# A fused mixture-of-experts kernel on one Trainium2 core: an expert's down products in seven half-size products for eight, from the third pair of batch rows on

## The chip, the core and the metric

The kernel runs on one core of a Trainium2 chip. Its engines work side by side, each through its own queue in order: PE (matrix products; its weight loads are shown apart as PEld), DVE, ACT and POOL (elementwise work), and SP, which issues the DMAs. They share SBUF; PE writes its products to PSUM, which DVE and ACT can read. The metric is the device time of one execution in microseconds (us), smaller being better.

## The reference, cut to what matters

Four layers are applied to `x` of shape (16, 256, 256), each added to `x`: L0, a mixer with 16 exponential moving averages per batch row and some small matrix products; L1, an attention pooling; L2, nine experts (eight and a shared one) with gated hidden layers of 1024; L3, a hidden layer of 1024 whose last 64 output columns come from one expert per batch row. All is fp32. The change is in L2:

```python
g = jnp.einsum('bsd,edf->ebsf', h, Wg)
u = jnp.einsum('bsd,edf->ebsf', h, Wu)
expert_outs = jnp.einsum('ebsf,efd->ebsd', jax.nn.silu(g) * u, Wd)
expert_output = jnp.einsum('be,ebsd->bsd', gating_probs, expert_outs)
```

## The kernel before

**Pairs and positions.** L2 and L3 take batch rows in pairs (512 columns). The work is a plan of positions 0 to 44; position `pos` takes expert `pos % 9`. Pair 0 rides from position 0 (its two rows at first apart), pair 1 from 9 to 17, pair 2 from 14 to 22, pair 3 from 18 to 26, pair 4 from 23 to 31, pair 5 from 27 to 35, pair 6 from 32 to 40, pair 7 from 36 to 44. So most positions serve two pairs with one load of weights, and positions 41 to 44 one pair. After a pair's last expert comes its L3. One pair at one position is called a *unit* here.

**A unit** (`l2_unit`) goes through 8 chunks of 128 hidden values. Every fp32 product is taken in three passes (`mm3`, lines 102 to 104), from a rounded high part and a low part of both operands. Per chunk, PE takes gate and up (4 products of three passes, 512 columns) into PSUM tiles `pg`, `pu`; ACT takes the SiLU (line 744), DVE multiplies (745, one operand `pu` in PSUM), ACT rounds the high part (89), POOL subtracts for the low part `hh` (96). Then `down` takes two products of three passes of 512 columns into `y0`, `y1`. `down` is put on PE two chunks later (`LAG`). At the end of an expert, DVE adds `y` into `acc` with four instructions (line 792).

**Weights** come in chunks of 768 columns into a ring of 10 tiles. On its first two uses a chunk is loaded raw and split by ACT and DVE (or POOL); on the second it is stored in `keep_e`, and from then on loaded ready (line 666).

**L0 and L1** of batch row b (`traces(b)`, `pooled(b)`) are cut into steps, which `pace` lays between the chunks, so that each row is done before its pair boards. Rows 6 to 15 are worked on while positions 14 to 35 run. One row has 16 averages: for each, DVE multiplies a gate by a modulation (line 328, twice 256 columns), DVE scans it (332, twice), POOL adds it up (336). The gate tile `gp` lies in PSUM (`ps_a`), and so do the factors `decay` of the scans (`ps_l`); the other operands `mod` and `bt` lie in SBUF:

```python
decay = ps_l.tile([P, ND + 1], F32, tag="decay", name="decay")
...
ga = ps_a.tile([P, 2, S], F32, tag="ga", name=f"gp{b}")
```

PSUM has eight banks: three for `pg`/`pu`, two for `y0`, `y1`, one each for `gp`, `decay` and L0's products. The instructions of each engine stand in an order that a scheduler fixed when the kernel was built; each waits by semaphores.

Of the kernel before, what the change touches and what calls it, by code (L numbers as in the profile page):

```python
# [8 lines left out]
F32 = mybir.dt.float32  # L9
# [11 lines left out]
NE = 8  # L21
# [5 lines left out]
L0_BUFS = {"bt": 3, "tr": 3, "mod": 2, "hA": 2, "hB": 2}  # L27
SECOND = 9
APART = 5
STORE = 2  # L30
LAG = 2
BOOST = 400
HOLD = 3
# [12 lines left out]
def fused_kernel(  # L46
# [23 lines left out]
    cp = ctx.enter_context(tc.tile_pool(name="const", bufs=1))  # L70
    xin = ctx.enter_context(tc.tile_pool(name="xin", bufs=2))
    l0 = ctx.enter_context(tc.tile_pool(name="l0", bufs=1))
    ring = ctx.enter_context(tc.tile_pool(name="ring", bufs=RING))
    raws = ctx.enter_context(tc.tile_pool(name="raws", bufs=2))
    xs = ctx.enter_context(tc.tile_pool(name="xs", bufs=3))
    accp = ctx.enter_context(tc.tile_pool(name="accp", bufs=3))
    hp = ctx.enter_context(tc.tile_pool(name="hp", bufs=2))
    dram = ctx.enter_context(tc.tile_pool(name="dram", bufs=2, space=bass.MemoryType.DRAM))
    keep = ctx.enter_context(tc.tile_pool(name="keep", bufs=1, space=bass.MemoryType.DRAM))
    ps_gu = ctx.enter_context(tc.tile_pool(name="ps_gu", bufs=3, space=PSUM))  # L80
# [87 lines left out]

    decay = ps_l.tile([P, ND + 1], F32, tag="decay", name="decay")
    V.reciprocal(decay, alpha)  # L170

    bmx = cp.tile([P, 2], F32, name="bmx")
    V.tensor_reduce(bmx, bl, AX.X, ALU.max)
# [26 lines left out]
    G.iota(jrow, [[P, 2]], base=1, channel_multiplier=1)  # L200

    def later_constants():

        V.tensor_copy(vr[:, 0:1], vec[:, V_V : V_V + 1])
        low("v", vr[:, 1:2], vec[:, V_V : V_V + 1], vr[:, 0:1])
        V.tensor_copy(n2[:, 0, :], vec[:, V_WN2 : V_WN2 + 48])
        low("v", n2[:, 1, :], vec[:, V_WN2 : V_WN2 + 48], n2[:, 0, :])

        V.tensor_copy(cnt[:, 0], jrow)
        V.tensor_scalar(cnt[:, 1], cnt[:, 0], -1.0, S + 1.0, ALU.mult, ALU.add)  # L210
        V.memset(cnt[:, 2], S - 1.0)
        V.tensor_copy(ptf, pti)
        V.tensor_scalar(flag[:, 0], ptf, 0.0, None, ALU.is_equal)
        V.tensor_scalar(flag[:, 1], ptf, 1.0, None, ALU.is_equal)
        V.tensor_tensor(flag[:, 2], flag[:, 0], flag[:, 1], ALU.add)
        V.tensor_scalar(flag[:, 2], flag[:, 2], -1.0, 1.0, ALU.mult, ALU.add)

        V.tensor_scalar(kindf, flag[:, 0], -2.0, 2.0, ALU.mult, ALU.add)
        V.tensor_tensor(kindf, kindf, flag[:, 1], ALU.subtract)
        V.tensor_copy(kind_i, kindf)  # L220
        for t in range(3):
            o = cntb if t == 0 else ctmp
            V.tensor_tensor(
                o,
                flag[:, t].unsqueeze(2).to_broadcast([P, NB, 2]),
                cnt[:, t].unsqueeze(1).to_broadcast([P, NB, 2]),
                ALU.mult,
            )
            if t:
                V.tensor_tensor(cntb, cntb, ctmp, ALU.add)  # L230
# [29 lines left out]

    def traces(b):

        xr = xin_tiles.pop(b)
        xh, xl = hl(f"x_{b}", "hA")
        rnd("a", xh, xr)
# [29 lines left out]
        yield  # L295
        pg = ps_l.tile([P, 2, S], F32, tag="ps", name=f"pg{b}")

        ga = ps_a.tile([P, 2, S], F32, tag="ga", name=f"gp{b}")
        for m in range(2):
            for k in range(4):  # L300
                o = O_G + k * S + m * P
# [352 lines left out]
    ring_tiles = {}  # L654

    kept, seen_of = {}, {}

    def load_chunk(key):  # L660
        kind = key[0]
        again = (kind, key[2])
        if kind != "c" and again in kept:
            t = ring.tile([P, 2, 768], F32R, tag="w", name="w_" + "_".join(map(str, key[:2])) + f"_{key[-1]}")
            n = 768 if kind == "e" else 384
            nc.sync.dma_start(t.bitcast(F32)[:, :, :n], kept[again])
            ring_tiles[key] = t
            return
        raw = raws.tile([P, 768], F32, tag="raw", name="raw_" + "_".join(map(str, key)))
        t = ring.tile([P, 2, 768], F32R, tag="w", name="w_" + "_".join(map(str, key[:2])) + f"_{key[-1]}")  # L670
        if kind == "e":
            n = 768
            nc.sync.dma_start(raw, wexp[key[2]])
        elif kind == "f":
            n = 384
            nc.sync.dma_start(raw[:, :n], w3[key[2]])
        else:
            n = 512
            b, i = key[1], key[2]
            nc.sync.dma_start(  # L680
                raw[:, :520],
                comb[bass.ds(eregs[b], 1), i].rearrange("o p c -> (o p) c"),
            )
            if i == 0:
                V.tensor_copy(bias3[:, b : b + 1], raw[:, 512:513])
        rnd("a", t[:, 0, :n], raw[:, :n])
        e = "v"
        if kind == "e" and key[1] == 0:

            e = "g" if key[2] < 2 else "v" if key[2] < 6 else "gv"[key[2] % 2]  # L690
        elif kind == "e" and key[1] < ALONE and key[2] % 3 == 0:
            e = "g"
        low(e, t[:, 1, :n], raw[:, :n], t[:, 0, :n])
        ring_tiles[key] = t
        seen_of[again] = seen_of.get(again, 0) + 1
        if kind == "e" and seen_of[again] == STORE or kind == "f":
            d = keep.tile([P, 2, n], F32, name="keep_" + "_".join(map(str, again)))
            nc.sync.dma_start(d, t.bitcast(F32)[:, :, :n])
            kept[again] = d

    eregs = {}


    x2_tiles = {}
# [34 lines left out]
    y_of = {}  # L739

    def hidden(ps_g, ps_u, uid, bias=None):
        h = hp.tile([P, 512], F32, tag="h", name=f"h{uid}")
        if ps_u is not None:
            A.activation(h, ps_g, AF.Silu)  # L744
            last_of["h"] = V.tensor_tensor(h, h, ps_u, ALU.mult)  # L745
        else:
            A.activation(h, ps_g, AF.Gelu, bias=bias)  # L747
        t = hp.tile([P, 2, 512], F32R, tag="hh", name=f"hh{uid}", bufs=3)
        rnd("a", t[:, 0], h)
        low("g", t[:, 1], h, t[:, 0])  # L750
        return t
# [5 lines left out]
    def l2_unit(pos, cis, bs):  # L757
# [39 lines left out]

        st2.push(down)

    def l3_chunk(p, f):  # L800
        uid[0] += 1
        xt = x2_tiles[p]
        w = ring_tiles[("f", p, f)]
        q = ps_gu.tile([P, 512], F32, tag="gu", name=f"q_{uid[0]}")
        for k in range(2):
            ws = slice(k * P, (k + 1) * P)
            mm3(q, w[:, 0, ws], w[:, 1, ws], xt[:, 0, k], xt[:, 1, k], k == 0, k == 1)
        t = hidden(q, None, uid[0], bias=vec[:, V_L3B1 + f : V_L3B1 + f + 1])
        u = uid[0]
# [1 line left out]
        def down():  # L811
            if f == 0:
                y_of[0] = [ps_y.tile([P, 512], F32, tag=f"y{m}", name=f"z{m}_{u}") for m in range(2)]
            mm3(y_of[0][0], w[:, 0, 256:384], w[:, 1, 256:384], t[:, 0], t[:, 1], f == 0, f == NF - 1)
            for i in range(2):
                b = 2 * p + i
                cw = ring_tiles[("c", b, f // 4)]
                ws = slice((f % 4) * P, (f % 4 + 1) * P)
                ts = slice(i * S, (i + 1) * S)
                mm3(  # L820
                    y_of[0][1][:, ts], cw[:, 0, ws], cw[:, 1, ws], t[:, 0, ts], t[:, 1, ts],
                    f == 0 and i == 0, f == NF - 1 and i == 1, skip_group_check=True,
                )
            if f == NF - 1:
                a = acc_tiles[p]
                V.scalar_tensor_tensor(a[:, 0], y_of[0][0], vec[:, V_B2 : V_B2 + 1], a[:, 0], ALU.add, ALU.add)  # L826
                nc.sync.dma_start(out[p, :, 0], a[:, 0])
                for i in range(2):
                    b = 2 * p + i
                    ts = slice(i * S, (i + 1) * S)  # L830
                    V.scalar_tensor_tensor(  # L831
                        a[:, 1, ts], y_of[0][1][:, ts], bias3[:, b : b + 1], a[:, 1, ts], ALU.add, ALU.add
                    )
                nc.sync.dma_start(out[p, :, 1], a[:, 1])
# [16 lines left out]
    for pos in range(max(r[1] for r in rides)):  # L851
        e = pos % NX
        units = [r[2] for r in rides if r[0] <= pos < r[1]]
        for ui, bs in enumerate(units):
            for b in bs:
                boards.setdefault(b, len(plan))
            step = 2 // len(bs)
            for c in range(e * NF, (e + 1) * NF, step):
                cis = list(range(c, c + step))
# [1 line left out]
                plan.append(("l2", (pos, cis, bs), keys, keys if ui == len(units) - 1 else [], 4))  # L861
        for p in ends.get(pos, []):
            for f in range(NF):
                keys = [("f", p, f)] + [("c", b, f // 4) for b in (2 * p, 2 * p + 1)]
                plan.append(("l3", (p, f), keys, keys if f % 4 == 3 else keys[:1], 3))

# [8 lines left out]
    def prefetch(n, boost=BOOST):  # L875
        while n > 0 and nxt[0] < len(order):
            k = order[nxt[0]]
            if k[0] == "c" and k[1] not in eregs:
                eregs[k[1]] = nc.sync.value_load(eix[0:1, k[1] : k[1] + 1], min_val=0, max_val=NE - 1)
            with tc.high_priority(offset=boost) if boost else nullcontext():  # L880
                load_chunk(k)
            nxt[0] += 1
            n -= 1

# [98 lines left out]
    owed = 0.0  # L985
    for i, item in enumerate(plan):
        kind, args, _, done = item[:4]
        if kind == "l2":
            bs = args[2]
            while n_done[0] <= bs[-1]:  # L990
                step()
            l2_unit(*args)
        else:
            if args[0] not in x3_done:
                st2.flush()
# [7 lines left out]
        if not (soon[0] == "l3" and soon[1][1] < HOLD):  # L1003
            for _ in range(min(int(owed), int(rate) + 2)):
                step()
                owed -= 1
        prefetch(len(done))
    st2.flush()


# [107 lines left out]
```

## Time and profile before

| | us |
|---|---|
| three runs: median (lowest to highest) | 2840.7 (2838.91 to 2842.95) |
| the profiled execution: time | 2841.92 |
| the profiled execution: span of its instructions | 2840.2 |
| PE busy in the span | 2779.2 |
| DVE, POOL, ACT busy in the span | 1425.2, 1299.0, 1235.4 |

Busy time is the time in which at least one instruction of the engine runs; PE's products overlap in a pipeline, so that the distance from start to start says more than the duration of one. The difference of 1.7 us between time and span lies around the program. Idle time before a group of instructions is shown with what ended it ("<-"). DVE's idle time does not cost anything as long as PE does not wait for it.

### The profile page before, as it was taken

The page shows a single profiled execution, that of the slowest core. Times are in us where ns is not written, and L with a number is a line of the kernel's source. Part 1 is how long each engine was busy: PE and PEld are TensorE (multiplying, and loading weights), DVE is VectorE, ACT ScalarE, POOL GpSimd, SP SyncE. Part 2 cuts the span into 40 slices and gives each one's busy share as a digit, 9 for nine tenths or more (in the row PEclk, how much of TensorE's full clock was granted, in tenths as well). Part 3 has the DMA queues.
Part 4 walks back from the last instruction along what each step waited for, and adds up shares of the span by engine and source line. Part 5 has one row for each costly group of instructions (what it writes and reads, how often), then busy time and mean ns, then how long its engine had stood idle before and what let it go on. Part 6 is the DMA issues. An engine that isn't in the chain of part 4 may idle for free. (4 is left out here: it accounts for less than half of the span.)

```text
span 2840.2 us, 36878 instructions
## 1 busy us (share of the span) xinstructions
PE 2779.2 (98%) x13604; PEld 2335.0 (82%) x13604; DVE 1425.2 (50%) x2646; ACT 1235.4 (43%) x2043; POOL 1299.0 (46%) x986
## 2 busy tenths in 40 slices
PE   7889989999999999999999999999999999999998
PEld 4877779888888888888888888888888888888887
DVE  7888766665665364544545445453444542222222
ACT  5555544546444533435334443334433453323433
POOL 5764654544544353544534445444444443333333
PEclk9999999999999999999999999999999999999999
DMA  4444645546443533324433153331523242222552
GB/s 125 136 148 122 196 162 181 185 131 230 148 164 117 180 115 104 119 77 135 150 110 106 40 180 112 111 117 58 177 101 112 91 169 90 89 89 76 192 198 83
DMA packets 114693, 371.23 MB, mean 131 GB/s; under 512 B 12642, under 2 KB 30930, under 8 KB 114514
## 3 DMA queue, kind: packets, MB, share of 16 engines
q1 hardware_dynamic: 114082, 368.82, 39.2%
q8 instruction: 108, 1.77, 0.3%
q14 instruction: 71, 0.58, 0.1%
q10 hardware_dynamic: 432, 0.06, 0.0%
HBM read 304.62 MB, written 64.21 MB: 130 GB/s over the span
## 5 line engine op out<-in xcount | busy, mean ns | idle before, releaser
L96 POOL TENSOR_TENSOR hh<-h,hh 128x512 fp32r<-128x512 f32 x640 | 848.7, 1326 | 1317.4 <-ACT hh L89 1297.4
L745 DVE TENSOR_TENSOR h<-h,pu 128x512 f32<-128x512 f32 x576 | 393.5, 683 | 941.9 <-PE pu L104 813.0
L89 ACT ACTIVATE hh<-h 128x512 fp32r<-128x512 f32 x640 | 403.4, 631 | 936.0 <-DVE h L745 914.9
L744 ACT ACTIVATE h<-pg 128x512 f32<-128x512 f32 x576 | 342.8, 595 | 317.7 <-PE pg L104 236.5
L102 PE MATMUL pg<-x,w_e 128*128 128x512 f32 (+1 forms) x1232 | 466.3, 379 | 10.1 <-ACT h L744 3.9
L102 PE MATMUL pu<-x,w_e 128*128 128x512 f32 (+1 forms) x1232 | 464.9, 377 | 7.5 <-ACT h L744 7.4
L104 PE MATMUL pg<-x,w_e 128*128 128x512 f32 (+1 forms) x1232 | 465.3, 378 | 1.8 <-DVE w_e L96 1.4
L103 PE MATMUL y<-hh,w_e 128*128 128x512 f32 (+1 forms) x1232 | 463.7, 377 | 2.5 <-POOL hh L96 2.5
L103 PE MATMUL pg<-x,w_e 128*128 128x512 f32 (+1 forms) x1232 | 464.7, 377 | 0.8 <-POOL x L96 0.8
L103 PE MATMUL pu<-x,w_e 128*128 128x512 f32 (+1 forms) x1232 | 463.7, 376 | 0.0
L104 PE MATMUL pu<-x,w_e 128*128 128x512 f32 (+1 forms) x1232 | 463.7, 376 | 0.0
L104 PE MATMUL y<-hh,w_e 128*128 128x512 f32 (+1 forms) x1232 | 463.1, 376 | 0.0
L102 PE MATMUL y<-hh,w_e 128*128 128x512 f32 (+1 forms) x1232 | 415.2, 377 | 2.9 <-ACT hh L89 1.6
L336 POOL TENSOR_TENSOR ta<-ta,tr 128x512 f32<-128x512 f32 x225 | 308.9, 1373 | 84.4 <-DVE tr L332 72.1
L332 DVE TENSOR_TENSOR_SCAN tr<-decay,bt 128x256 f32<-128x256 f32 x450 | 284.7, 669 | 0.0
L102 PEld LDWEIGHTS pg<-x,w_e 128*128 128x128 f32 x1232 | 232.5, 189 | 53.1 <-ACT h L744 4.8
L102 PEld LDWEIGHTS pu<-x,w_e 128*128 128x128 f32 x1232 | 232.6, 189 | 51.2 <-ACT h L744 9.9
L103 PEld LDWEIGHTS y<-hh,w_e 128*128 128x128 f32 x1232 | 232.8, 189 | 46.3 <-POOL hh L96 4.6
L104 PEld LDWEIGHTS pg<-x,w_e 128*128 128x128 f32 x1232 | 232.7, 189 | 44.9 <-DVE w_e L96 2.4
L102 PEld LDWEIGHTS y<-hh,w_e 128*128 128x128 f32 x1232 | 231.5, 189 | 45.7 <-ACT hh L89 2.6
L104 PEld LDWEIGHTS y<-hh,w_e 128*128 128x128 f32 x1232 | 232.7, 189 | 41.8
L104 PEld LDWEIGHTS pu<-x,w_e 128*128 128x128 f32 x1232 | 232.5, 189 | 41.9
(279 smaller groups left out, 3220.8 us busy)
## 6 DMA issues: line engine op xcount, KB each, us to landing
w_e<-keep_e SPq DMA_DIRECT2D x216, 768.0 KB, 4.4
raw_e<-in_wexp_dram SPq DMA_DIRECT2D x144, 384.0 KB, 4.3
keep_e<-w_e SPq DMA_DIRECT2D x72, 768.0 KB, 4.3
mod<-mdd SPq DMA_DIRECT2D x120, 256.0 KB, 3.7
w_f<-keep_f SPq DMA_DIRECT2D x56, 384.0 KB, 3.5
raw_c<-in_comb_dram SPq DMA_DIRECT2D x32, 260.0 KB, 2.8
xr<-in_xT_dram SPq DMA_DIRECT2D x16, 256.0 KB, 3.7
xt<-in_x_dram SPq DMA_DIRECT2D x16, 256.0 KB, 2.7
```

Source lines behind the costliest of these rows:

```text
L89: last_of["ca"] = A.activation(out_, in_, AF.Copy)
L96: i = (V if e == "v" else G).tensor_tensor(out_, in_, h.bitcast(F32), ALU.subtract)
L102: PE.matmul(o, wh, xh, start=start, stop=False, **kw)
L103: PE.matmul(o, wh, xl, start=False, stop=False, **kw)
L104: last_of["pe"] = PE.matmul(o, wl, xh, start=False, stop=stop, **kw)
L332: V.tensor_tensor_scan(tr[:, c], decay[:, d : d + 1].to_broadcast([P, S]), bt[:, c], 0.0, ALU.mult, ALU.add)
L336: G.tensor_tensor(tacc, tacc, tr, ALU.add)
L744: A.activation(h, ps_g, AF.Silu)
L745: last_of["h"] = V.tensor_tensor(h, h, ps_u, ALU.mult)
```

## The change

From position 14 on, a unit is taken in steps j of two chunks (256 hidden values), each in two halves (`half_unit`). Gate and up are as before: 24 passes of 512 columns per j. The down product is a product of 2 by 2 blocks (two chunks by two rows of the pair; 128 by 128 weights, 256 columns), and it is taken in seven block products for eight: 21 passes of 256 columns, where 12 passes of 512 stood. For that,

- the hidden values are combined by three subtractions on DVE (tile `t`), and seven blocks of 256 are split in high and low parts (b11, b2, t13, t24) where four were;
- the weights get four sums per j (DVE, once per expert, positions 14 to 22), and are kept as two tiles per j, `g` (1024 columns) and `d` (896), in pools of three each. A second pair takes the j in reverse order, and loads j = 0 anew;
- there are four accumulators `y0` to `y3` instead of two. `y2` and `y3` take the PSUM banks of `gp` and `decay`; for rows from 6 on (`LATE`), the gate tile (`gs`) and the factors (`decay_late`) lie in SBUF;
- at the end of an expert ACT copies one block, and DVE runs two additions and five multiply-adds, where it ran four;
- `down` of one j stands behind the gate and up products of the next.

The pools of the ring (`ring`, `raws`, `hp`) are closed at position 14, and the new pools (`lw`, `lraw`, `lh`) are laid in their space. Before position 14, chunks are no longer stored.

```diff
+SEVEN = 14
+LATE = 6
...
+    decays = {False: decay, True: cp.tile([P, ND + 1], F32, name="decay_late")}
...
+        V.tensor_copy(decays[True], decay)
...
+        decay = decays[b >= LATE]
...
-        ga = ps_a.tile([P, 2, S], F32, tag="ga", name=f"gp{b}")
+        ga = ps_a.tile([P, 2, S], F32, tag="ga", name=f"gp{b}") if b < LATE else ft("ga", f"gs{b}")
...
+    def parts(t, c0, src, n):
+        rnd("a", t[:, 0, c0 : c0 + n], src)
+        low("v", t[:, 1, c0 : c0 + n], src, t[:, 0, c0 : c0 + n])
...
+            if kind == "g":
+                parts(t, 0, r0[:, :512], 512)
+                parts(t, 512, r1[:, :512], 512)
+            else:
+                a11, a21, a12, a22 = r0[:, 512:640], r0[:, 640:768], r1[:, 512:640], r1[:, 640:768]
+                sums = pools["lh"].tile([P, 4, P], F32, tag="s", name=f"sums_{e}_{j}", bufs=1)
+                V.tensor_tensor(sums[:, 0], a21, a22, ALU.add)
+                V.tensor_tensor(sums[:, 1], sums[:, 0], a11, ALU.subtract)
+                V.tensor_tensor(sums[:, 2], a11, a21, ALU.subtract)
+                V.tensor_tensor(sums[:, 3], a12, sums[:, 1], ALU.subtract)
+                parts(t, 0, a11, P)
+                parts(t, P, r1[:, 512:768], 2 * P)
+                parts(t, 3 * P, sums.rearrange("p a b -> p (a b)"), 4 * P)
...
+        def split(tag, src, n, bufs):
+            t = lh.tile([P, 2, n], F32R, tag=tag, name=..., bufs=bufs)
+            rnd("a", t[:, 0], src)
+            low("g", t[:, 1], src, t[:, 0])
+            return t
...
+        A.activation(part, pg, AF.Silu)
+        last_of["h"] = V.tensor_tensor(part, part, pu, ALU.mult)
+        if i == 0:
+            hid["b11"] = split("b", h[:, 0], S, 2)
+            return
+        t = lh.tile([P, 4, S], F32, tag="t", name=f"t{u}", bufs=1)
+        V.tensor_tensor(t[:, 0:2], h.rearrange("p (c n) s -> p c n s", n=2)[:, :, 1], h[:, 0:2], ALU.subtract)
+        V.tensor_tensor(t[:, 2], h[:, 3], t[:, 0], ALU.subtract)
+        V.tensor_tensor(t[:, 3], h[:, 2], t[:, 2], ALU.subtract)
...
+        b2 = split("hh", flat[:, 512:1024], 512, 3)
+        t13 = split("hh", tf[:, 0:512], 512, 3)
+        t24 = split("hh", tf[:, 512:1024], 512, 3)
...
+                    (y0[:, 0], True, 0, b11, 0),
+                    (y1[:, 0], True, 1, b2, 0),
+                    (y2[:, 0], True, 6, b2, 1),
+                    (y2[:, 1], False, 3, t13, 0),
+                    (y3[:, 0], True, 5, t13, 1),
+                    (y0[:, 1], False, 4, t24, 0),
+                    (y1[:, 1], False, 2, t24, 1),
...
+                A.activation(s[:, 0], y0[:, 0], AF.Copy)
+                V.tensor_tensor(s[:, 1], s[:, 0], y0[:, 1], ALU.add)
+                V.tensor_tensor(s[:, 2], s[:, 1], y3[:, 0], ALU.add)
+                add(acc[:, :, :S], y1, ca)
+                add(acc[:, :, S:], y2[:, 1:2].to_broadcast([P, 2, S]), cb)
+                add(acc[:, 0, S:], y2[:, 0], cb)
+                add(acc[:, :, S:], s[:, 1:3], cb)
+                add(acc[:, :, :S], s[:, 0:3:2], ca)
...
+        st2.flush()
+        st2.push(down)
```

## The prediction

> **What bounds the kernel now.** First the page's sums and its costliest groups (busy time, mean ns of one | idle time before them):
>
> ```profile
> PE 2779.2 (98%) x13604; PEld 2335.0 (82%) x13604; DVE 1425.2 (50%) x2646; ACT 1235.4 (43%) x2043; POOL 1299.0 (46%) x986
> ...
> L96 POOL TENSOR_TENSOR hh<-h,hh 128x512 fp32r<-128x512 f32 x640 | 848.7, 1326 | 1317.4 <-ACT hh L89 1297.4
> L745 DVE TENSOR_TENSOR h<-h,pu 128x512 f32<-128x512 f32 x576 | 393.5, 683 | 941.9 <-PE pu L104 813.0
> ...
> L336 POOL TENSOR_TENSOR ta<-ta,tr 128x512 f32<-128x512 f32 x225 | 308.9, 1373 | 84.4 <-DVE tr L332 72.1
> L332 DVE TENSOR_TENSOR_SCAN tr<-decay,bt 128x256 f32<-128x256 f32 x450 | 284.7, 669 | 0.0
> ```
>
> PE is the bound; DVE waits for PE, POOL for ACT. Then the same by stage: positions 0 to 13, 14 to 22, 23 to 35, 36 to 44, cut at the end of the last layer-3 block of each (the stretch, then PE, PEld, DVE, ACT, POOL busy, granted clock, DMA share, GB/s):
>
> ```profile
> 0.00:666.00 666.00, 616.00 (x3470) 525.58 (x3471) 486.92 (x868) 359.02 (x598) 369.13 (x269) 0.97 0.50 158
> 666.00:1352.00 686.00, 684.33 (x3258) 574.09 (x3257) 361.07 (x687) 305.46 (x505) 320.17 (x244) 1.00 0.40 134
> 1352.00:2333.00 981.00, 979.09 (x4628) 821.03 (x4627) 460.33 (x894) 399.01 (x666) 444.17 (x346) 1.00 0.34 115
> 2333.00:2840.00 507.00, 499.73 (x2254) 414.32 (x2253) 116.86 (x201) 171.87 (x277) 165.55 (x128) 1.00 0.36 120
> ```
>
> Where the change acts, PE hardly rests; what it saves there would come straight off the time, if nothing else becomes the bound. I call the three late stages A (686 us), B (981) and C (507).
>
> **What PE saves.** The timeline of PE shows start times where products of 512 and of 256 columns follow each other:
>
> ```profile
> 437.84 0.39 PE L103 MATMUL pu<-x,w_e 128*128 128x512 f32 x1
> 438.06 0.39 PE L104 MATMUL pu<-x,w_e 128*128 128x512 f32 x1
> 438.29 0.28 PE L102 MATMUL y<-hh,w_e 128*128 128x256 f32 x1
> 438.40 0.28 PE L103 MATMUL y<-hh,w_e 128*128 128x256 f32 x1
> 438.52 0.28 PE L104 MATMUL y<-hh,w_e 128*128 128x256 f32 x1
> ```
>
> Long runs give 0.227 us per 512 columns and 0.1195 per 256 (twelve of these from 438.29 to 439.72). A group (one j of one pair) has 12 x 0.227 = 2.72 us of down products before and 21 x 0.1195 = 2.51 after: 0.214 less. There are 58 pairs-at-a-position from 14 on, with 4 groups each: 232 x 0.214 = 50 us. The first 512 behind a run of 256 starts 0.24 later instead of 0.227, some 6 us in all. So PE's own saving is 44 to 50 us, and a unit goes from 8 x 18 x 0.227 = 32.7 us to 31.8. [...]
>
> **What the other engines get, and the port.** These two answers of the timeline decide my forecast. In the first, DVE scans (factor `decay` in PSUM) while POOL works: two scans take 1.26 us, as ever. In the second, DVE's operands both lie in SBUF: it starts 0.48 us behind POOL and ends 0.55 us after POOL's end; alone it takes 0.69.
>
> ```profile
> 1499.81 1.30 POOL L96 TENSOR_TENSOR hh<-h,hh 128x512 fp32r<-128x512 f32 x1 [0.61 <-ACT hh L89]
> 1500.10 1.26 DVE L332 TENSOR_TENSOR_SCAN tr<-decay,bt 128x256 f32<-128x256 f32 x2
> ```
>
> ```profile
> 1995.84 1.29 POOL L96 TENSOR_TENSOR hh<-h,hh 128x512 fp32r<-128x512 f32 x1 [3.04 <-ACT hh L89]
> 1996.32 1.36 DVE L96 TENSOR_TENSOR w_c<-raw_c,w_c 128x512 fp32r<-128x512 f32 x1 [0.54 <-ACT w_c L89]
> ```
>
> ```profile
> L96 DVE TENSOR_TENSOR w_c<-raw_c,w_c x32: 662/1057/1783, 592.0 to 2808.8; 128x512 fp32r<-128x512 f32 x32
> L366 DVE SCALAR_TENSOR_TENSOR g<-g,sm x15: 678/684/1425, 129.9 to 2295.2; 128x512 f32<-128x512 f32 x15
> ```
>
> I took every place in the trace where one DVE instruction with both operands in SBUF overlaps one POOL instruction (96): from the first start to the last end it takes the two durations alone, added, less 0.13 us (80% of them between 0.11 and 0.16). They exclude each other. DVE instructions with an operand in PSUM show nothing of it: 155 multiplies `h<-h,pu` beside POOL take 0.677 us, 421 alone 0.688. [...]
>
> So POOL's time plus DVE's time with both operands in SBUF must fit into each stage ("port time"). Durations: POOL 1.29 (median) per 512 columns, 0.71 per 256 (the weight split of 256 columns at the start); DVE 0.68 per 512, 0.42 per 256, some 0.28 per 128 (extrapolated), scans 0.633 and `bt` 0.432 back to back (284.7/450, 207.5/480).
>
> - A unit: POOL splits 3 blocks of 512 and one of 256 per j, 4 x 4.58 = 18.3 us (before 8 x 1.29 = 10.3). DVE's `t`, 0.68 + 2 x 0.42 per j, gives 6.1, and two multiply-adds from `s` 1.4 (before: none, `pu` and `y` are in PSUM). Port 25.8 against 10.3.
> - A batch row of layers 0 and 1: POOL 19 x 1.29 + 0.7 = 25.2. With gate and factors in SBUF, 34 scans (21.5) and 32 `bt` (13.8) join; small ones are 5.2. Port 65.7 against 29.7.
> - Layer 3 of a pair: POOL 10.3, DVE 4.1: 14.4, as before.
> - First preparation of a j's weights (positions 14 to 22, 36 of them): lows 0.68 x 3 + 0.42 + 0.28, four sums 1.12: 3.9 each.
>
> | stage | units, rows, layer-3 blocks | port before | port after | PE after |
> |---|---|---|---|---|
> | A | 18, 4, 2 (and 36 preparations) | 374 | 464 + 263 + 29 + 140 = 896 | 662 |
> | B | 26, 6, 3 | 483 | 671 + 394 + 43 = 1108 | 961 |
> | C | 14, 0, 2 | 171 | 361 + 29 = 390 | 489 |
>
> PE is 31.8 per unit, 11.3 per row (84 products of 256 and some small), 22 per layer-3 block; with 32.7 it gives 678, 984 and 502 for before, where the trace has 686, 981 and 507. In A and B the port needs more than PE: it becomes the bound. DVE's whole busy time in A, some 640 us, is close to PE's as well. Behind a blocked DVE instruction stand the multiplies `h<-h,pu` that PE's next down products need, so PE waits.
>
> The port sum isn't exact. A hand-over saves up to 0.13 us at either end of each POOL instruction (384 in A, 560 in B: 100 and 146 us at most). Against that, DVE's instructions with PSUM operands (8.3 us per unit, about 6 per row: 173 and 252 us) stand in the same queue, and cost whatever does not fall beside a POOL instruction. I let the two cancel, since POOL's 450 and 656 us leave room for most but not all. **Sum:** 2842 + (896 - 686) + (1108 - 981) - 14 x 0.86 in C = 3167.
>
> **The rest.** The switch of pools: the first raw load waits for the products that free the ring, and PE has some 3 to 8 us of work from there to its first use, against 4.3 us of landing and about 3 of splitting; four j's must be prepared in a row. I take 10 us (0 to 30). Loads: between the product that frees a tile of `g` or `d` and the first product on its successor stand mostly 15 to 20 us of PE work, above 8 everywhere; a kept tile lands in 4.4 us (768 KB; somewhat more for 1 MB), so nothing is late. For layer 3's `f2` there are only 2.5 to 9 us against 3.5: 5 us in all (0 to 20). Accumulators: between a pair's last down product and the next one's first stand 24 products (5.4 us), and the chain that reads `y` is 0.4 + 2 x 0.41 + 2 x 0.75 + 0.48 = 3.2; hidden in C, and inside the port's delay in A and B. In C, a j has 8.0 us of PE against 4.6 of POOL and under 5 of DVE: its saving arrives. **Forecast: 3182, say 3180 us**, counted from the profiled execution's 2841.9 (median of three 2840.7).
>
> **Rivals.** *Port-bound, as above:* hand-overs all saved gives 2842 + 110 - 22 (B is PE's again) - 12 + 15 = 2933, and with nearly a third of the PSUM instructions unhidden it is 3182 + 130 = 3310; chance 0.60 for 2970 to 3310. *Scans go free:* no row shows a scan with both operands in SBUF. If it doesn't exclude POOL, A loses 4 x 21.5 and B 129: 810 and 979, so 2842 + 124 - 2 - 12 + 15 = 2967, less half the hand-overs in A 2917; 0.18 for 2880 to 2970. *Worse:* engines in order pass the delay back and forth, with little overlap; everything in DVE's queue and POOL's one after the other would be 896 + 173 and 1108 + 252, 3600 in all; 0.09 above 3330. *The other side:* the exclusion doesn't hold for the new instructions. Then PE stays the bound, as DVE's sum alone (some 640 of 662 in A) just fits, and 2842 - 50 + 15 = 2807 results. This decides as soon as the port needs less than PE in both stages, that is, 234 us less in A; scans and `bt` together (141) are not enough, so `t` and the preparations would have to go free too. For it speaks only that no row shows these very instructions: 0.11. *The small products save nothing:* at 0.130 us each, 21 cost as much as 12 large ones, and with a free port 2842 remains; the rows say 0.1195: 0.02.
>
> Runs of this kernel tell a difference of about 0.2%. Chances: faster 0.11, same 0.02, slower 0.87. The range takes in the first two cases with a margin: 2880 to 3330.
>
> **What would show it.** In the changed profile, PE's busy share drops in A and B and not in C; scans (line 338) and `bt` (334) have means well above 0.67 and 0.47 us with maxima near 2; POOL's splits likewise rise above 1.29; PE waits for POOL `hh`, ACT `hh` and DVE `h`. Stage A ends some 200 us later against its start than before, B some 130, C some 10 earlier. Scans at 0.67 beside POOL would prove the forecast wrong, and PE at 98% everywhere the whole of it.

## The result and the profile after

The changed kernel takes 3203.3 us (median of four runs, 3198.1 to 3205.7), the kernel before, measured beside it, 2840.9. The ratio is 1.1273 (95% interval 1.1254 to 1.1293): 362 us more. The profiled execution has a span of 3202.8 us. The lines of its page that answer to those of before:

```profile
PE 2891.5 (90%) x15692; PEld 2452.2 (77%) x15692; DVE 2571.8 (80%) x3809; ACT 1490.1 (47%) x2714; POOL 1909.7 (60%) x1450
...
L338 DVE TENSOR_TENSOR_SCAN tr<-decay_late,bt 128x256 f32<-128x256 f32 x300 | 260.6, 899 | 0.0
...
L334 DVE SCALAR_TENSOR_TENSOR bt<-gs,bl,mod 128x256 f32<-128x256 f32 x320 | 255.9, 838 | 0.1
```

Before, the line of `bt` was:

```profile
L328 DVE SCALAR_TENSOR_TENSOR bt<-gp,bl,mod 128x256 f32<-128x256 f32 x480 | 207.5, 474 | 2.0 <-DMA mod<-mdd 1.8
```

DVE has gone from 50% to 80%, and its scans from 0.669 to 0.899 us, `bt` from 0.474 to 0.838. Now by stage (the stretch, then PE, PEld, DVE, ACT, POOL busy, granted clock, DMA share, GB/s), cut at the end of the same layer-3 blocks, to a microsecond or two:

```profile
0.00:663.00 663.00, 610.71 (x3443) 520.88 (x3443) 484.00 (x864) 351.86 (x589) 367.80 (x267) 0.97 0.35 105
663.00:1580.00 917.00, 769.97 (x3959) 639.08 (x3960) 815.24 (x1258) 428.75 (x827) 526.26 (x392) 0.94 0.45 159
1580.00:2698.00 1118.00, 1017.83 (x5549) 863.72 (x5548) 946.70 (x1286) 489.05 (x899) 717.56 (x554) 0.98 0.41 141
2698.00:3203.00 505.00, 493.02 (x2746) 428.53 (x2744) 325.84 (x404) 220.42 (x401) 298.03 (x239) 0.99 0.48 170
```

A grows from 687 to 917, B from 980 to 1118, C stays (506 and 505). In A DVE is busy for 815 of 917 us, PE for 770. PE's waits over the whole span (us in total, times, longest):

```profile
PE pg L105 <- DVE h L901: 67.7, 45, 4.9
PE y L105 <- ACT hh_t L92: 52.9, 61, 3.6
PE pu L105 <- ACT h L900: 30.2, 26, 3.0
PE y L105 <- DVE acc L954: 26.4, 22, 2.7
PE y L106 <- POOL hh_t L99: 26.0, 40, 1.5
```

PE waits all along one chain: the SiLU and the multiply of `h`, the split of the sums `t`, the accumulators. The first and the third line (98 us) aren't waits for data: `pg` and `pu` share three PSUM buffers (`ps_gu`), and the next gate or up product needs one that the multiply or the SiLU has read. What holds the chain up is seen in the timeline, where two scans with both operands in SBUF stand beside one POOL split: 2.25 us for the split (1.29 alone) and 2.32 for the scans (1.26 with `decay` in PSUM).

```profile
1709.36 2.25 POOL L99 TENSOR_TENSOR hh_h<-h,hh_h 128x512 fp32r<-128x512 f32 x1 [1.03 <-ACT hh_h L92]
1709.84 2.32 DVE L338 TENSOR_TENSOR_SCAN tr<-decay_late,bt 128x256 f32<-128x256 f32 x2
```

The waits are not the whole loss. PE's timeline after a wait:

```profile
705.71 0.79 PE L107 MATMUL pg<-x,w_g 128*128 128x512 f32 x1 [1.45 <-DVE w_g L99]
706.30 0.63 PE L105 MATMUL pg<-x,w_g 128*128 128x512 f32 x1
706.73 0.63 PE L106 MATMUL pg<-x,w_g 128*128 128x512 f32 x1
...
708.86 0.51 PE L105 MATMUL pu<-x,w_g 128*128 128x512 f32 x1
709.21 0.40 PE L106 MATMUL pu<-x,w_g 128*128 128x512 f32 x1
```

From 706.30 to 708.86 products of 512 columns start 0.43 us apart, and then 0.23 again. So I split PE's time in the three late stages into products at their undisturbed distance (0.2266 and 0.1195 us), waits, and the rest, slow products: 2112 + 253 + 173 us after the change; before it, 2154 + 7 + 9. The products' time falls by 42 us (counted at fixed distances, so this isn't a measured saving yet; e10 below measures it); 246 us of waits and 164 of slow products come. Of the 173 us some 70 lie where the granted clock reads 0.5. Most of the others belong to the waits: idle time counts only from the end of the product before, 0.39 us after its start (0.28 for 256 columns), so a start behind a wait comes another 0.16 us late (273 times, 46 us), and shorter holds aren't counted as waits at all (some 41 us).

### The profile page after: what moved, and what is told of

The parts are those of the page before. It is cut to its first block, busy times and chain, and to the rows that moved or that the text cites. A ratio compares the mean times of both kernels' runs of the same rounds, so it can differ in the third digit from the quotient of the medians.

```text
span 3202.8 us, 43824 instructions
## 1 busy us (share of the span) xinstructions
PE 2891.5 (90%) x15692; PEld 2452.2 (77%) x15692; DVE 2571.8 (80%) x3809; ACT 1490.1 (47%) x2714; POOL 1909.7 (60%) x1450
## 3 DMA queue, kind: packets, MB, share of 16 engines
q8 instruction: 123, 2.02, 0.3%
## 5 line engine op out<-in xcount | busy, mean ns | idle before, releaser
L99 POOL TENSOR_TENSOR hh_t<-t,hh_t 128x512 fp32r<-128x512 f32 x464 | 658.0, 1422 | 257.1 <-ACT hh_t L92 244.0
L92 ACT ACTIVATE hh_t<-t 128x512 fp32r<-128x512 f32 x464 | 292.1, 630 | 566.5 <-DVE t L910 270.2
L99 POOL TENSOR_TENSOR hh_h<-h,hh_h 128x512 fp32r<-128x512 f32 x232 | 346.8, 1495 | 267.9 <-ACT hh_h L92 254.3
L105 PE MATMUL pg<-x,w_g 128*128 128x512 f32 x928 | 383.2, 413 | 79.9 <-DVE h L901 67.7
L105 PE MATMUL pu<-x,w_g 128*128 128x512 f32 x928 | 378.4, 408 | 33.2 <-ACT h L900 30.2
L99 POOL TENSOR_TENSOR hh<-h,hh 128x512 fp32r<-128x512 f32 x176 | 243.9, 1387 | 243.3 <-ACT hh L92 215.0
L107 PE MATMUL pg<-x,w_g 128*128 128x512 f32 x928 | 374.2, 403 | 5.5 <-DVE w_g L99 5.4
L106 PE MATMUL pg<-x,w_g 128*128 128x512 f32 x928 | 375.4, 405 | 0.0
L106 PE MATMUL pu<-x,w_g 128*128 128x512 f32 x928 | 372.2, 401 | 0.0
L107 PE MATMUL pu<-x,w_g 128*128 128x512 f32 x928 | 370.2, 399 | 0.0
L99 POOL TENSOR_TENSOR b_h<-h,b_h 128x256 fp32r<-128x256 f32 x232 | 207.3, 893 | 134.5 <-ACT b_h L92 130.0
L105 PE MATMUL y<-hh_t,w_d 128*128 128x256 f32 x928 | 238.4, 295 | 53.8 <-ACT hh_t L92 52.9
L106 PE MATMUL y<-hh_t,w_d 128*128 128x256 f32 x928 | 259.8, 293 | 26.4 <-POOL hh_t L99 26.0
L338 DVE TENSOR_TENSOR_SCAN tr<-decay_late,bt 128x256 f32<-128x256 f32 x300 | 260.6, 899 | 0.0
L334 DVE SCALAR_TENSOR_TENSOR bt<-gs,bl,mod 128x256 f32<-128x256 f32 x320 | 255.9, 838 | 0.1
L107 PE MATMUL y<-hh_t,w_d 128*128 128x256 f32 x928 | 253.8, 287 | 0.0
```

The source lines that it names most:

```text
L92: last_of["ca"] = A.activation(out_, in_, AF.Copy)
L99: i = (V if e == "v" else G).tensor_tensor(out_, in_, h.bitcast(F32), ALU.subtract)
L105: PE.matmul(o, wh, xh, start=start, stop=False, **kw)
L106: PE.matmul(o, wh, xl, start=False, stop=False, **kw)
L107: last_of["pe"] = PE.matmul(o, wl, xh, start=False, stop=stop, **kw)
L334: V.scalar_tensor_tensor(bt[:, c], ga[:, c], bl[:, c, d : d + 1], mod[:, d % 2], ALU.mult, ALU.mult)
```

## The experiments

What each gave, with A and B read from its own profile (cut as above), and two shares of those stages: DVE's busy time (in it the time that a started instruction is held up), and the time in which POOL or a DVE instruction with two SBUF operands runs, counted from both timelines ("port"). The last column ("`h` held") is the mean time by which DVE starts a multiply `h` after both its inputs, the SiLU and the last product of `pu`, are there.

| run | time, us | ratio (95%) | A, us (DVE, port) | B, us (DVE, port) | `h` held in A, B, us |
|---|---|---|---|---|---|
| before | 2840.9 | 1 | 687 (53%, 52%) | 980 (47%, 48%) | 0.27, 0.18 |
| after | 3203.3 | 1.1273 (1.1254 to 1.1293) | 917 (89%, 87%) | 1118 (85%, 86%) | 3.04, 1.87 |
| e1_psum_both | 3073.3 | 1.0808 (1.0790 to 1.0826) | 869 (86%, 78%) | 1035 (81%, 78%) | 2.13, 1.30 |
| e1a_factors_psum | 3130.9 | 1.1016 (1.0997 to 1.1034) | 889 (88%, 81%) | 1081 (83%, 80%) | 2.56, 1.63 |
| e1b_gate_psum | 3152.4 | 1.1088 (1.1068 to 1.1108) | 889 (90%, 85%) | 1097 (83%, 83%) | 2.65, 1.75 |
| e2_move_only | 2861.7 | 1.0070 (1.0053 to 1.0086) | 706 (63%, 68%) | 979 (59%, 65%) | 0.58, 0.36 |
| e3_low_on_act | 3008.8 | 1.0591 (1.0573 to 1.0609) | 812 (89%, 79%) | 1031 (80%, 72%) | 2.02, 1.20 |
| e4_both | 2929.6 | 1.0314 (1.0297 to 1.0331) | 782 (86%, 66%) | 982 (76%, 57%) | 1.61, 0.80 |
| e5_from_36 | 2909.3 | 1.0241 (1.0224 to 1.0258) | 686 (53%, 52%) | 974 (47%, 48%) | 0.29, 0.18 |
| e6_no_prep | 3101.4 | 1.0915 (1.0897 to 1.0934) | 806 (84%, 85%) | 1118 (85%, 86%) | 1.83, 1.87 |
| e7_all_free | 2863.7 | 1.0074 (1.0057 to 1.0091) | 709 (75%, 56%) | 981 (76%, 58%) | 0.75, 0.79 |
| e8_no_sums | 2983.9 | 1.0496 (1.0479 to 1.0514) | 819 (86%, 87%) | 1000 (70%, 84%) | 2.11, 1.05 |
| e9_limit | 2853.9 | 1.0040 (1.0027 to 1.0054) | 701 (54%, 45%) | 976 (53%, 46%) | 0.22, 0.28 |
| e10_pe_only | 2800.2 | 0.9852 (0.9837 to 0.9867) | 674 (53%, 53%) | 961 (48%, 49%) | 0.23, 0.14 |

**Where operands lie.** Three kernels bring the scan factors, the gate or both back into PSUM; instructions and sizes stay. To free the banks, outputs share accumulators. The diff shows both moves together (e1_psum_both).

```diff
-        decay = decays[b >= LATE]
+        decay = decays[False]
...
-        ga = ps_a.tile([P, 2, S], F32, tag="ga", name=f"gp{b}") if b < LATE else ft("ga", f"gs{b}")
+        ga = ps_a.tile([P, 2, S], F32, tag="ga", name=f"gp{b}")
...
-            y0, y1, y2, y3 = y_of[0]
+            y0, y1 = y_of[0]
+            y2, y3 = y1, y0
...
```

> The changed kernel, but gate and scan factors stay in PSUM for all rows; to free the banks, y2 is accumulated in y1's bank and y3 in y0's (so from pair 14 on the sums of two outputs are mixed up: the amount of work is that of the changed kernel, the values are not). Theory (SBUF exclusion between DVE and POOL is what costs): scans and bt of the late rows leave the port, so port time falls from 911 to 748 us in A and from 1102 to 878 in B (PE 663 and 955): A about 750 to 790, B 960 to 990, scans back to 0.67 us, whole time 2900 to 2960, about 2930. Rival (the longer chain from pu over t, split and a or b to the down products is what costs, wherever the operands lie): that chain is untouched, so the time stays above 3150.

> Only the scan factors stay in PSUM for all rows, with y3 accumulated in y0's bank (their values are mixed up, the amount of work is the same); the gate is in SBUF as in the changed kernel. Theory: port 815 us in A and 970 in B: A about 820, B about 985 to 1000, whole time about 2990. Rival (only the chain of the seven products counts): above 3150.

> Only the gate stays in PSUM for all rows, with y2 accumulated in y1's bank (values mixed up, same amount of work); the scan factors are in SBUF as in the changed kernel. Theory: port 844 us in A and 1010 in B: A about 850, B about 1025, whole time about 3040 to 3070. If the scan doesn't exclude POOL as bt does, it should be e1a that gains nothing and this one that gains all: then below 2960.

Measured: 130, 72 and 51 us less than after, and 72 + 51 is nearly 130. Scans and `bt` are undisturbed again in e1, and in e1a and e1b each where its own operand has moved:

```profile
L338 DVE TENSOR_TENSOR_SCAN tr<-decay,bt 128x256 f32<-128x256 f32 x450 | 286.1, 670 | 0.0
L334 DVE SCALAR_TENSOR_TENSOR bt<-gp,bl,mod 128x256 f32<-128x256 f32 x480 | 207.2, 473 | 2.0 <-DMA mod<-mdd 1.8
```

```profile
L338 DVE TENSOR_TENSOR_SCAN tr<-decay,bt 128x256 f32<-128x256 f32 x450 | 287.4, 670 | 0.0
L334 DVE SCALAR_TENSOR_TENSOR bt<-gs,bl,mod 128x256 f32<-128x256 f32 x320 | 250.0, 820 | 0.8 <-DMA mod<-mdd 0.6
```

```profile
L338 DVE TENSOR_TENSOR_SCAN tr<-decay_late,bt 128x256 f32<-128x256 f32 x300 | 296.3, 1022 | 0.0
L334 DVE SCALAR_TENSOR_TENSOR bt<-gp,bl,mod 128x256 f32<-128x256 f32 x480 | 207.0, 473 | 3.4 <-DMA mod<-mdd 3.2
```

These runs show the exclusion for scan and `bt` alike: with both operands in SBUF a scan takes 0.90 us (after) and 1.02 (e1b) on average, with `decay` in PSUM 0.67 (e1, e1a); `bt` takes 0.84 (after) and 0.82 (e1a), with `gp` in PSUM 0.47 (e1, e1b). Apart from the shared accumulators only the place of two operands differs; so their place costs some 130 us. But I expected 270 (and about 213 and 133 to 163 of e1a and e1b). A went to 869, not 750 to 790, B to 1035, not 960 to 990. The rival, that place doesn't matter, falls too; neither explains that the port is now 78% busy and PE still waits.

**The move alone.** The first two edits of that diff the other way round, in the kernel before.

> The kernel before with one thing alone: gate and scan factors move to SBUF from the seventh row on; no product in seven, no other pools. Theory: port time rises from 365 to 528 us in A and from 483 to 706 in B, still under PE's 686 and 981: the scans get longer (about 0.9 us mean) but the time stays within 2840 to 2865. Rival (SBUF operands cost by themselves, because a blocked DVE passes each delay on to PE): up to 163 + 223 us of added port time reach the end, 2900 to 3035.

```profile
PE 2788.2 (98%) x13604; PEld 2336.0 (82%) x13604; DVE 1622.9 (57%) x2647; ACT 1230.4 (43%) x2043; POOL 1342.1 (47%) x986
...
L336 DVE TENSOR_TENSOR_SCAN tr<-decay_late,bt 128x256 f32<-128x256 f32 x300 | 286.9, 994 | 0.0
```

The scans are longer still (0.994 us, 0.9 expected) than in the changed kernel, and the whole costs 20 us, within the theory's range. The held-up scans and `bt` cost little here, where DVE had room: 19 us in A, with DVE 63% busy, and nothing in B, at 59%.

**POOL's load.**

```diff
...
-            low("g", t[:, 1], src, t[:, 0])
+            if act:
+                rnd("a", t[:, 1], src)
+            else:
+                low("g", t[:, 1], src, t[:, 0])
...
```

> The changed kernel, but the low parts of t1,t3 and t2,t4 are written by ACT as a second rounding of the whole value in place of POOL's subtraction (the low parts are thereby wrong; products and their number are unchanged). Two of POOL's four splits per j go, 2 x 1.29 us, and ACT gets 2 x 0.63. Theory (the port is the bound): port time 725 us in A and 834 in B, PE 663 and 955: A 730 to 750, B 960 to 985, whole time about 2880. Rival (the cost is in DVE's queue or in the SBUF operands of the rows alone): scans still as long as before and a gain of less than 100 us, above 3100.

> Both of the former: gate and factors in PSUM with y2 and y3 accumulated in the banks of y1 and y0 (values mixed up), and the low parts of t1,t3 and t2,t4 written by ACT (wrong low parts). Port time 562 and 610 us, under PE everywhere. Theory: PE is the bound again and shows what the seven products save when nothing hinders them: 2810 to 2835 us; near 2835 if the products of 512 stay at 0.2306 us mean in place of 0.2266, which in the last stage ate 11 of 12 us. Rival (PE's whole saving of 44 to 50 us comes through): 2797 to 2813.

e3: 195 us less, with A at 812 (expected 730 to 750) and B at 1031 (960 to 985). It also shortens the chain from `t` to the products (0.63 us on ACT for 1.29 on POOL), so it doesn't show the port alone. e4: 2930, not 2810 to 2835; port time 66% and 57%, and A still 108 us above what PE alone takes there (674, in e10 below). So a full port is not what bounds A. DVE's share fits better: it stayed between 84 and 90% in A in all of after, e1, e1a, e1b, e3, e4, e6 and e8, while the port's went from 87 to 66%. And what A lost in length is about what DVE lost in busy time: 48 us of length and 69 of busy time in e1, 105 and 96 in e3, 135 and 141 in e4. The last column of the table shows the queue itself: a multiply `h` that could start stands 3.04 us on average in A after the change, for 0.27 before, and DVE works on something else in nearly all of that time (scans 83 of 444 us in all, the splits and sums of the weights, `t`, `bt`). Over the runs this delay falls about as the length of A and B does.

**Seven products only where no rows are left.**

```diff
-SEVEN = 14
-LATE = 6
+SEVEN = 36
+LATE = 16
...
```

> The changed kernel with the seven products only from position 36 on, that is for the last 14 units, where no rows of layers 0 and 1 are left; gate and factors never move, and the weights of earlier units come as in the kernel before. The 36 preparations of weights fall into the last stage. Theory: stages A and B are as in the kernel before; in C the port needs 523 us (383 and 36 times 3.9) against PE's 492: C 525 to 545, whole time 2860 to 2880. Rival (PE alone counts there): 2832 to 2840.

```profile
2328.00:2906.00 578.00, 527.40 (x2776) 440.45 (x2776) 477.77 (x736) 296.73 (x585) 307.62 (x241) 0.98 0.57 205
```

```profile
PE pg L106 <- DVE h L910: 12.4, 14, 1.5
PE pg L106 <- ACT w_g L93: 6.1, 4, 2.5
```

C takes 578 us, more than the 525 to 545 expected (the whole 2909, 2860 to 2880 expected): no scan is left there, but the 36 preparations bring DVE to 83%, and a multiply `h` stands 1.77 us in C, for 0.11 before. My second theory took shape here: the bound is DVE's queue in order, whose length is its own work plus what the exclusion adds; PE waits for `h` behind whatever DVE does at that time.

**The preparations, and all three together.**

```diff
...
-            r0, r1 = raw_pair(e, j)
...
+            c0, m = (0, 512) if kind == "g" else (320, 448)
+            for i in range(2):
+                src = kept["e", e * NF + 2 * j + i]
+                nc.sync.dma_start(t.bitcast(F32)[:, :, i * m : (i + 1) * m], src[:, :, c0 : c0 + m])
```

> The changed kernel without the preparations of the late weights: the parts that earlier positions (5 to 13) have rounded are stored there, and the late positions load them; the four sums per j are left out and other columns stand in their place (w_d is wrong, its size and number of products are not). Port work in A falls by 36 times 3.9 = 140 us. Theory (port use alone counts): A falls from 917 to between 775 and 830, B and C stay at 1118 and 502, whole time about 3080. Rival (in A the preparations cost more than their port time, since DVE and ACT run them in a row ahead of what PE needs; the two earlier changes together still left A 119 us above PE): A falls to 750 or below. Second rival (they fall into gaps): less than 70 us gained.

> No preparations (as in e6_no_prep), gate and factors in PSUM, and the low parts of t1,t3 and t2,t4 written by ACT (as in e4_both; outputs are wrong as told there). Port work 422 us in A, 610 in B, 244 in C. Theory (what was left in A of e4_both was the preparations): A 670 to 695, B 982, C 499, whole time 2810 to 2835, the first time that seven products are faster than eight. Rival (the longer chain from pu over t and split to the down products costs the rest): A stays above 750, whole time above 2890.

e6: A 806 and B 1118, as expected (the whole 3101, about 3080 expected); DVE lost 134 us in A, and A 111. e7: 2864 where 2810 to 2835 was expected, A 709 against 670 to 695; of the miss, 10 us come ahead of A (670 us, 660 in e4), where this kernel adds stores. With DVE at 75% PE is the bound again, yet the time isn't below that of before.

**The three sums per j.** `t` goes; the splits read `h`.

> The changed kernel without the three sums t per j on DVE: the two splits read h in their place (wrong values, same splits and products). Port work falls by 6.1 us per unit: 110 in A, 158 in B, and the chain to the last down products gets shorter by three instructions. If each us of port work were a us of time, A 805, B 960, whole time 2935. In the runs so far a us less of port work gave 0.3 to 0.6 us; by that A 850 to 885, B 1025 to 1070, whole time 3040 to 3105. Above 3150 the sums would have been hidden.

```profile
L338 DVE TENSOR_TENSOR_SCAN tr<-decay_late,bt 128x256 f32<-128x256 f32 x300 | 309.4, 1065 | 0.0
...
L334 DVE SCALAR_TENSOR_TENSOR bt<-gs,bl,mod 128x256 f32<-128x256 f32 x320 | 267.7, 875 | 0.1
```

219 us less, between the two expectations. Scans and `bt` are even longer than after, the port's share is as high (84 to 87%), and B is 118 us shorter: the length of a scan by itself is not the cost. `t` takes 6.1 us of port time per unit, and gives back 0.89 us (A) and 0.75 (B) per us; the rows' operands gave 0.29 and 0.37 (e1). `t` stands in the chain from `pu` to PE's next products, a scan only in the queue ahead of it. Whether the shorter chain or DVE's shorter queue (113 us less in A) makes most of the gain, this run doesn't separate. The delay of `h` falls to 2.11 and 1.05 us here, in e1 to 2.13 and 1.30; for about the same delay in A, e1 gained 48 us there and e8 98, which speaks for a part of the chain's own.

**PE's part alone, and the limit.** In the kernel before:

```diff
...
+                    for i in range(2 if pos >= 14 else 0):
+                        hs = slice(i * S, (i + 1) * S)
+                        if m + i < 2 or f not in (1, 3, 5, 6):
+                            mm3(
+                                y_of[0][m][:, hs], w[:, 0, ws], w[:, 1, ws], t[:, 0, hs], t[:, 1, hs],
+                                f == 0 and i == 0, f == NF - 1, skip_group_check=True,
+                            )
...
```

> The kernel before with PE's part of the change alone: from position 14 on, each down product of 512 columns is issued as two of 256, and one of the eight block products per two chunks is left out (its part of the output is missing); 21 products of 256 for 12 of 512 in each of 232 groups. Nothing else is touched. My prediction's saving, 44 to 50 us, would give 2791 to 2798. With 512-column products at 0.2295 us (mean of the undisturbed ones in e7_all_free) in place of 0.227, the 5568 of them that are left in the late stages cost 14 us, and about 2810 is expected. If small products saved nothing, 2840.

> e7_all_free, and the three sums t are left out as well (as in e8_no_sums): nothing of the change is left that asks more of DVE and POOL than one more split of a block per j and the longer end of an expert; ACT has more. Theory (what is left over in e7_all_free, 709 us in A against 663 for PE, is DVE's queue ahead of PE): A 680 to 695, B 965 to 978, C 493 to 498, whole time 2825 to 2845, 10 of which are the stores ahead of A that this experiment adds. Rival (it is PE's own order and tails): within 5 us of e7_all_free's 2864.

The stages of e10, PE's part alone:

```profile
668.00:1342.00 674.00, 672.91 (x3910) 593.66 (x3909) 359.71 (x688) 305.68 (x504) 321.02 (x245) 1.00 0.41 137
1342.00:2303.00 961.00, 961.00 (x5563) 847.90 (x5562) 458.02 (x892) 401.39 (x665) 443.95 (x346) 1.00 0.35 117
2303.00:2800.00 497.00, 489.75 (x2750) 427.75 (x2748) 116.33 (x198) 171.25 (x276) 164.51 (x128) 1.00 0.36 123
```

Alone, seven products for eight save 41.6 us: 13 in A, 19 in B, 9 in C. All that stands around them costs 403. e9 took 2854, 9 us above its range and 10 below e7: so DVE's queue was only a small part of what e7 had left over (A 709 to 701, B 981 to 976). Even without sums, preparations, moved operands and two of POOL's splits, something that remains (the longer end of an expert, the new loads and pools, ACT's extra work, that kernel's own stores) eats more than the 42 us. The runs don't share it out; PE's two longest waits in e9's late stages are for loads, 10.5 us for `w_g` and 9.5 for layer 3's `w_f`:

```profile
PE pg L105 <- DMA w_g<-keep_e: 10.5, 2, 7.8
```

So no partial repair of this change was found that is faster than before; with 42 us to win there is little room for one.

## Why the prediction was right, and where it wasn't

- **Sign, size and place were right.** 3180 was forecast, 3203 came; A 896 (917 came), B 1108 (1118). Scans and `bt` at 0.90 and 0.84 us with single ones up to 1.79, PE's waits for `h` and `hh`, and A growing by more than B came as announced. "Scans go free" and "the exclusion doesn't hold" are refuted by the page, and by e1, e1a and e1b for each operand.
- **"The port becomes the bound" failed as a step.** The hand-overs saved nearly all that they could, if the whole difference is theirs: port time was 801 us in A and 964 in B, 95 and 144 less than the sums (at most 100 and 146 were named). But the port was idle for the rest, 116 and 154 us: the 173 and 252 us of PSUM instructions, set against the hand-overs as a guess, came out between nothing and all. Two terms of about 100 to 150 us cancelled as guessed, and that the sum came so close is luck to this extent. The runs with less port work show it: by the port's rule e1 and e3 should have given 2930 and 2880, and gave 3073 and 3009. In place of it they showed DVE's queue (`h` held for 3.04 us in A, for 0.27 before): the line "DVE's whole busy time in A, some 640 us, is close to PE's as well" came nearest to it, and I didn't add to it what the exclusion adds (815 us in all).
- **The path to PE was half named.** The prediction let PE wait for the inputs of its down products; the listed waits of that kind are 90 us. As many, 98 us, came by the PSUM buffers that the next gate and up products need.
- **The waits cost PE more than themselves.** The prediction has no term for the half clock (granted 0.5 in 37 stretches, 0.43 us from start to start for 512 columns), in which PE's products lost some 70 us. (The 173 us of slow products, 21 in e10, hold that and the edges of the waits.)
- **PE's saving** of 44 to 50 us was 42 (e10). The term "first 512 behind a run of 256, some 6 us" was mis-sized: not the first alone but the first five start 0.229 to 0.235 us apart, so that the undisturbed mean is 0.2298 us in e10 for 0.2273 before. Time beyond the undisturbed distances is 21 us in e10 for 9 before: 12 where the term had 6.
- **C:** "its saving arrives" failed. 12 us were forecast, 1 came; PE's part alone gives 9 (e10). The rest went in waits of 7.6 us for 3.0 before (3.7 for the input of the last layer 3, 1.2 before, and 2.8 for `hh_t`) and in slow products (9 us, 5 in e10).
- **Preparations:** 140 us of port time were forecast; without them A is 111 us shorter (e6).
- **Accumulators** were called hidden in C, which held, and inside the port's delay in A and B; there PE waits for them 22 times, 26 us in all. The argument of 5.4 against 3.2 us holds only where DVE runs free.
- **Small terms:** waits for the first late weights are 14 us (10 forecast with the pool switch), for `f2` 0.7 (5 forecast).

## What to carry to other kernels

Here, work that left the bound engine was paid for on the others (42 us saved on PE alone, 403 lost around them), and DVE's queue counted with the time it was held up: 815 us busy in A, where its own work alone was some 640 by the prediction's estimate. So add what an exclusion that the trace shows lengthens to the queue, and don't wait for 100%. Here a stage with seven products took 15 to 39 us more than PE's part alone (674 and 961 us) with DVE 53 to 76% busy, and 70 to 243 us more with DVE 80 to 90% busy. Ask of each added instruction whether the bound engine waits for it: 300 scans held up for 0.3 us each, with as many `bt`, cost 20 us where DVE had room, while leaving out three small sums per step, which stand in the chain, gave 219 where it had none. Try the saving by itself first: 42 us was the most that could be won here.

## What the runs showed of the hardware

After some of its waits PE's products ran at half pace (0.43 us from start to start for 512 columns, 0.23 otherwise), and the record of the granted clock in the trace shows it: it reads 0.5 from 705.7 to 709.1 us, and in 37 such stretches in all in the late stages of the changed kernel up to its last products, each 3.4 to 10.2 us long. In the kernel before it reads 0.5 in none of the three stages until the last products are done. In the changed kernel's record all 37 begin whole multiples of 3.41 us apart. In the 3.41 us just ahead of each PE stood idle for 1.6 to 3.1 us, added up over its waits; of the some 650 late windows of this grid with the full clock in them and behind them none had more than 1.8 us of it. Ahead of 705.7 us the idle time is 2.4 us, of two waits of 1.1 and 1.45 us with a few products between them (702 to 706 us), each below those 1.8 us. In the stretches at 0.5 PE's products lost 49 us in A and 20 in B, beside 147 and 100 us of counted waits; the granted clock of A falls to 0.94 from 1.00.

Products of 512 columns behind a run of 256 started 0.229 to 0.235 us apart for the first five, and 0.226 to 0.228 from the sixth on (e10); with the many short runs of this order that is 0.2298 on average in e10 (6017 products with the next start within 0.26 us and no idle time between) against 0.2273 before (8789).
